# Weights behind the first preparation, its evictions on two engines, and a sort wait for every node-row DMA

## The chip, the cores and the metric

The kernel runs on one core of a Trainium2 chip. The metric is device time in microseconds, lower is better. The engines of the core are named PE (TensorE), DVE (VectorE), ACT (ScalarE), POOL (GpSimd) and SP (SyncE); each executes its own instructions in a fixed order, and waits for the others by semaphores.

## The reference

There are 16 graphs of 1024 nodes with 64 channels, and a dense 0/1 adjacency of each (about 16 neighbours a node). Two layers follow one another, both on normalized input. The first takes, for every node and channel, weighted quartiles over the node's remaining neighbours; the second is three graph convolutions.

```python
h = jnp.maximum(_layernorm(x, axis=-1), 0.0)
...
neigh = (adj_ > 0) & ~eye
...
skip = jnp.where(nb > T, (nb + K - 1) // K, 1)      # T, K = 10, 2
...
rem = neigh & (sk > 1) & (rank % sk == sk - 1) & mask[:, :, None]
rem = rem | jnp.swapaxes(rem, 1, 2)
adj_d = jnp.where(rem, 0.0, adj_)
nd = adj_d > 0
vals = jnp.where(nd[..., None], x[:, None, :, :], jnp.inf)
s = jnp.sort(vals, axis=2)
...
for tau, w in zip(TAUS, WTS):                       # quartiles 0.25, 0.5, 0.75
    ...
    agg = agg + jnp.asarray(w, x.dtype) * (v_lo + frac * (v_hi - v_lo))
...
h = jax.nn.relu(out @ W1 + b1)                      # out = x + agg
y = h @ W2 + b2
...
# second layer, adj undiminished
x1 = _bn(_gcn(x, adj, W1, b1), g1, be1, m1, v1)     # _gcn: relu(adj @ (x @ W) + b)
x2 = _bn(_gcn(x1, adj, W2, b2), g2, be2, m2, v2)
x3 = _bn(_gcn(x2, adj, W3, b3), g3, be3, m3, v3)
return jax.nn.relu(jnp.concatenate([x1, x2, x3], axis=-1) @ Wl + bl)
```

## The kernel before

The graphs are worked on in eight pairs. Three kinds of work follow one another for a pair.

*Preparation* (`prepare`, and `prepare_one` for each of its two graphs). The normalized rows are written to DRAM (h_d, and rows_d, which the node fetches read). Eight tiles of 128 rows of the adjacency are loaded by SyncE (L775, 512 KB each, two buffers), turned to fp8 by ScalarE with a count (edge, L782) and by VectorE (one, L786); PE transposes them (L789) and the result leaves PSUM as edgeT (L792, ScalarE). VectorE takes out the diagonal (L799), PE forms sums of every 128 columns (L757) and running counts (cs, L829 and L834), ScalarE and VectorE turn these into the removed edges (stays, L838 and L839), PE symmetrizes them (q, L849 to L860), and ScalarE evicts q as the remaining edges with the number of each node (L865). Nodes are then ordered by their number of neighbours: a key per node is spread over all partitions by PE (keys, L876), and eight comparisons with accumulation on ScalarE (L884) count how many keys lie above; `place` (L887) is the position. GpSimd scatters the edges' rows to their places in DRAM (live_d, L895) and reads them back (lp, L910), PE transposes them, ScalarE evicts (liveT, L933), and a list of source rows is drawn up: eight times row words on ScalarE (L988), a cast of every second pair (L993), and on VectorE the search for the largest numbers (L712, L714), which ends with rows_listed (L732). At the end the normalized rows are read again (h_again, L695) and split into three bf16 parts (hp, L697 to L700).

*Gathering and sorting.* The nodes in their new order are split into blocks. For most blocks PE gathers the neighbours' values by one-hot matrices that VectorE makes (s L1151 and L1216, pg L1176 and L1247), ScalarE evicts, and VectorE sorts them by a network of minima and maxima (L1092). For the three blocks of NODES, GpSimd fetches the neighbours' rows one slot at a time by indirect DMA (g_nodes, L1361, 744 in all); a DMA for a slot serves 128 nodes, and in one block there is one for each of `G` graphs or pairs, numbered by `a`.

*The layers* (`later`, `next_layer`). The sorted result goes through DRAM to its nodes' original order by indirect DMA of GpSimd (agg, L1554), VectorE adds it (L1451), and the two layers run on PE, ScalarE and VectorE (L1440 to L1532).

The order of the work is written by generators: `weave` interleaves the preparation of the next pair with the sorts of this one in shares (SHARES), and all layers with the sorts of the last pair (LATE_SHARES). The preparation of the first pair stands alone at the start: `ahead = Steps(prepare(0, early))`, `ahead.rest()`. From this program a list scheduler makes the fixed order of each engine; a dependency that carries no semaphore (NoSync) only constrains this order.

Ahead of the first preparation stand the constants. The weights are 48 DMAs, all issued by ScalarE (`weight`, `column`, `row`, `both`, L536 to L559), with three scale vectors made of them (bn_s, L571 to L577). GpSimd fills lines with values and sends them as a table of bounds (line L528, bounds L530, 32 DMAs). A tile `filler` with a zero row and a large row is set by VectorE (L623) in memory that the setup used before, and written by 16 ScalarE DMAs (L627) to the ends of rows_d.

A node-row DMA that is asked for during a sort gets a wait on the last instruction of that sort so far (`sorted_by`), but only for `a == 0`.

Of the kernel before, what the change touches and what calls it, by code (L numbers as in the profile page):

```python
# [10 lines left out]
F32 = mybir.dt.float32  # L11
# [397 lines left out]
def graph_layers_kernel(ctx: ExitStack, tc: tile.TileContext, ins, out: bass.AP):  # L409
# [126 lines left out]
    def weight(name, rows, cols, twice=False):  # L536
        t = const.tile([rows * (1 + twice), cols], F32, name=f"w_{name}")
        for k in range(1 + twice):
            nc.scalar.dma_start(out=t[k * rows : (k + 1) * rows, :], in_=ins[name])
        return t  # L540

    def column(name, rows, twice=False):
        t = const.tile([rows * (1 + twice), 1], F32, name=f"c_{name}")
        for k in range(1 + twice):
            nc.scalar.dma_start(out=t[k * rows : (k + 1) * rows, :], in_=ins[name].rearrange("(p o) -> p o", o=1))
        return t

    def row(name, cols):
        t = const.tile([P, cols], F32, name=f"r_{name}")
        nc.scalar.dma_start(out=t, in_=ins[name].partition_broadcast(P))  # L550
        return t

    def both(t, src):

        nc.vector.memset(t, 0.0)
        for k in range(2):
            half = slice(k * C, (k + 1) * C)
            nc.scalar.dma_start(out=t[half, half], in_=src)


    w1 = weight("L0_gnn_W1", C, HID, True)
    w2 = weight("L0_gnn_W2", HID, C)
    b1 = column("L0_gnn_b1", HID)
    b2 = row("L0_gnn_b2", C)
    layers = []
    for i in (1, 2, 3):
        wl = const.tile([P, P], F32, name=f"wl{i}")
        both(wl, ins[f"L1_gnn_W{i}"])
        bl, g, be, m, v = (column(f"L1_gnn_{k}{i}", C, True) for k in ("b", "g", "be", "m", "v"))
        s = const.tile([P, 1], F32, name=f"bn_s{i}")  # L570
        nc.vector.tensor_scalar(s, v, BN_EPS, None, ALU.add)  # L571
        nc.scalar.activation(s, s, AF.Sqrt)
        nc.vector.reciprocal(s, s)
        nc.vector.tensor_tensor(s, s, g, ALU.mult)

        nc.vector.tensor_tensor(m, m, s, ALU.mult)
        nc.vector.tensor_tensor(be, be, m, ALU.subtract)  # L577
        layers.append((wl, bl, s, be))
    wlast = const.tile([P, 3, P], F32, name="wlast")
    for i in range(3):  # L580
        both(wlast[:, i, :], ins["L1_gnn_Wl"][i * C : (i + 1) * C, :])
    blast = row("L1_gnn_bl", C)

# [37 lines left out]
    with tc.tile_pool(name="setup_fill", bufs=1) as setup:  # L621
        filler = setup.tile([2, C], F32, name="filler")
        nc.vector.memset(filler, BIG)  # L623
        nc.vector.memset(filler[:1, :], 0.0)
        for p in range(NP):
            for x in range(2):
                nc.scalar.dma_start(out=rows_d[p][x * ROWS + ZERO_ROW : x * ROWS + BIG_ROW + 1, :], in_=filler)  # L627

# [10 lines left out]
    def prepare(p, pools):  # L639
# [54 lines left out]
        for x in range(2):  # L694
            nc.sync.dma_start(out=h[:, x], in_=rows_of(h_d[2 * p + x][:, :]))  # L695
        st.hp = keep.tile([P, 3, 2, NT, C], BF16, tag="hp", name="hp")
# [68 lines left out]
    def prepare_one(st, x, pools, ahead=None):  # L765
        work, keep, ps = pools
        b = 2 * st.p + x
        mk = work.tile([P, NT], U8, tag="mk", name="mk")
        nc.sync.dma_start(out=mk, in_=mask_d[b])
# [10 lines left out]
        for t in range(NT):  # L780
            a, coming = coming, load(t + 1) if t + 1 < NT else None
            nc.scalar.activation(  # L782
                edge[:, t, :], a[:, :].bitcast(U32), AF.Sign, accum_out=found[:, 0, b, t : t + 1], saturate=False
            )
            one = work.tile([P, N], F8, tag="one", bufs=2, name="one")
            nc.vector.tensor_scalar(one, a, 1.0, None, ALU.is_equal, saturate=False)  # L786
            pt = ps.tile([P, NT, P], F32, tag="big", bufs=2, name="ptE")
            for u in range(NT):
                nc.tensor.matmul(  # L789
                    out=pt[:, u, :], lhsT=one[:, u * P : (u + 1) * P], rhs=ident_h, start=True, stop=True  # L790
                )
            nc.scalar.activation(  # L792
                edgeT[:, :, t * P : (t + 1) * P], pt, AF.Copy, accum_out=found[:, 1, b, t : t + 1], saturate=False
            )
            yield
# [48 lines left out]
        for t in range(NT):  # L844
            q = ps.tile([P, N], F32, tag="big", bufs=2, name="q")
            for hf in range(NH):
# [17 lines left out]

            nc.scalar.activation(  # L865
                edge[:, t, :], q, AF.Relu, bias=bias(-2.0), accum_out=nv[:, t : t + 1], saturate=False
            )
            yield
# [12 lines left out]

        junk = stays[:, 0, : N // 2].bitcast(F8)
        for t in range(NT):
            nc.scalar.activation(  # L884
                junk, keys, AF.Sign, bias=minus[:, t : t + 1], accum_out=above[:, t : t + 1], saturate=False
            )
        nc.vector.tensor_scalar(place[:, b, :], above, -0.5, 0.5 * (N - 1), ALU.mult, ALU.add)  # L887
# [34 lines left out]
        def find_live(lp_all, listed):  # L922
# [3 lines left out]
            for t in range(NT):  # L926
                lp = lp_all[:, t, :]
                pt = ps.tile([P, NT, P], F32, tag="big", bufs=2, name="pt")
                for u in range(NT):
                    nc.tensor.matmul(  # L930
                        out=pt[:, u, :], lhsT=lp[:, u * P : (u + 1) * P], rhs=ident_h, start=True, stop=True
                    )
                nc.scalar.activation(liveT[:, :, t * P : (t + 1) * P], pt, AF.Copy, saturate=False)  # L933
                yield
# [43 lines left out]
            for u in range(NT):  # L978
# [12 lines left out]
                if u % 2:  # L991
                    words = st.r[0][:, x, u - 1 : u + 1, :]
                    nc.scalar.copy(words, words.bitcast(BF16))  # L993
                    yield
# [353 lines left out]
    def fetch_nodes(pairs, i, pools, tag):  # L1348
# [7 lines left out]
        def ask():  # L1356
            for k in range(slots):
                for a in range(G):
# [7 lines left out]
                    )  # L1366
                    if a == 0 and sorted_by[0] is not None:
                        tc.add_manual_dep(
# [77 lines left out]
    def first_layer(pools, xt, h, agg, mask):  # L1446
# [7 lines left out]
        for x in range(X):  # L1454
            rows = slice(x * C, (x + 1) * C)
            hT = one.tile([HID, N], F32, tag="hT", name="hT")
            for hf in range(NH):
                sl = slice(hf * HALF, (hf + 1) * HALF)
                pm = ps.tile([HID, HALF], F32, tag="mm", name="pm1")
                nc.tensor.matmul(out=pm, lhsT=w1[rows, :], rhs=oT[rows, sl], start=True, stop=True)  # L1460
                nc.scalar.activation(hT[:, sl], pm, AF.Relu, bias=b1)
            py = ps.tile([P, NT, C], F32, tag="mm", name="py")
            for t in range(NT):
                nc.tensor.matmul(out=py[:, t, :], lhsT=hT[:, t * P : (t + 1) * P], rhs=w2, start=True, stop=True)  # L1464
            nc.vector.tensor_tensor(h[:, :, x, :], py, b2[:, None, :].to_broadcast([P, NT, C]), ALU.add)
            yield
# [7 lines left out]
    def next_layer(pools, graphs, adjT, x2, cur):  # L1474
# [6 lines left out]
        xs = []  # L1481
        for i, (wl, bl, s, be) in enumerate(layers):

# [35 lines left out]
        for hf in range(NH):  # L1519
            ts = slice(4 * hf, 4 * hf + 4)  # L1520
            pf = ps.tile([P, 4, X, C], F32, tag="mm", name="pf")
            for t in range(4):
                sl = slice((4 * hf + t) * P, (4 * hf + t + 1) * P)
                for i, xT in enumerate(xs):
                    nc.tensor.matmul(  # L1525
                        out=pf[:, t].rearrange("p x c -> p (x c)"), lhsT=xT[:, sl], rhs=wlast[:XC, i, :XC],
                        start=(i == 0), stop=(i == 2),
                    )
            nc.vector.tensor_tensor(
                res[:, ts], pf, blast[:, None, None, :].to_broadcast([P, 4, X, C]), ALU.add  # L1530
            )
# [212 lines left out]
    with ExitStack() as stack:  # L1744
# [6 lines left out]
        with ExitStack() as inner:  # L1751
# [4 lines left out]
            ahead = Steps(prepare(0, early))  # L1756
            ahead.rest()
            sts = [ahead.result]
            jobs = iter(NODE_ORDER)
# [132 lines left out]
```

## Time and profile before

| | |
|---|---|
| median of 3 runs | 2845.74 us (2841.83 to 2846.65) |
| the profiled execution, its own time | 2855.05 us |
| span of the profiled execution | 2853.2 us |
| mean granted TensorE clock | 0.869 |
| PE busy | 2127.4 us (75%), 21226 matmuls |
| DVE busy | 2259.9 us (79%), 5356 instructions |
| ACT busy | 1657.8 us (58%), 3324 |
| POOL busy | 1358.7 us (48%), 1155 |
| DMA traffic | 205.27 MB, mean 72 GB/s |

Times in the profile count from the start of the span. Busy time leaves out instructions that only issue a DMA on ACT and SP; these are shown on the engines' queues as ACTq and SPq. A row of a group gives its line, engine, operation, what it writes and reads, how many there are, busy time, the mean of one in ns, and the idle time of the engine just before them with what ended it. In the rows of slices a digit is a busy share in tenths.

### The profile page before, as it was taken

The numbers are of one execution on the slowest core, as the hardware profiler recorded it, in microseconds if no ns is written. First come the engines' busy times: TensorE is split into PE (matmuls) and PEld (weight loads), VectorE is DVE, ScalarE is ACT, GpSimd is POOL, SyncE is SP. The second block draws the span as 40 slices with busy tenths as digits, with TensorE's granted clock in tenths as the row PEclk, the third lists the DMA queues.
The fourth block names the chain that finished last, engine by engine and source line by source line (L and its number), as shares of the span: only waits on it lengthen the run. The fifth ranks groups of instructions, "written<-read, shape, count | busy, mean of one in ns | idle before, by whom it ended". The sixth has DMA issues, their size and how long they took to land. (4 is left out here: it accounts for less than half of the span.)

```text
span 2853.2 us, 54558 instructions
## 1 busy us (share of the span) xinstructions
PE 2127.4 (75%) x21226; PEld 1374.2 (48%) x21226; DVE 2259.9 (79%) x5356; ACT 1657.8 (58%) x3324; POOL 1358.7 (48%) x1155
## 2 busy tenths in 40 slices
PE   1567986897798699779855986997588496448768
PEld 0344563564455365545523553665355363234445
DVE  3117999889899989989999999989688486647843
ACT  2686788678677858867773777687423141122222
POOL 5115363475526416443734274175646748862220
PEclk9788997998899799789878997998798798778989
DMA  3303222322422323142431222322310351221221
GB/s 96 109 30 98 80 88 65 104 80 58 107 72 86 81 91 91 46 110 68 98 65 45 82 86 73 112 75 61 80 21 19 74 82 51 42 56 39 48 61 46
DMA packets 261035, 205.27 MB, mean 72 GB/s; under 512 B 217120, under 2 KB 217248, under 8 KB 256672
## 3 DMA queue, kind: packets, MB, share of 16 engines
q1 hardware_dynamic: 165120, 131.39, 15.5%
q0 software_dynamic: 39680, 62.23, 9.1%
q10 hardware_dynamic: 55968, 8.09, 2.1%
q8 instruction: 168, 2.75, 0.4%
q14 instruction: 99, 0.81, 0.1%
HBM read 148.82 MB, written 52.75 MB: 71 GB/s over the span
## 5 line engine op out<-in xcount | busy, mean ns | idle before, releaser
L1361 POOL DMA_INDIRECT g_nodes<-rows_d,rows_listed x744 | 979.2, 1316 | 952.5 <-DVE prod L1104 276.2
L1176 PE MATMUL pg<-s,hp 128*64 128x496 fp8e4 (+5 forms) x8064 | 747.0, 337 | 134.9 <-ACT hp L697 56.1
L1176 PEld LDWEIGHTS <-hp 128*64 128x64 bf16 x8064 | 450.2, 113 | 376.9 <-ACT hp L697 67.2
L1509 PE MATMUL pg<-adjT,xw 128*64 128x512 fp8e4 x2304 | 282.5, 394 | 24.6 <-ACT xw L1498 11.4
L895 POOL DMA_INDIRECT live_d<-edge,place x128 | 178.7, 1396 | 191.1 <-DVE place L887 154.9
L1151 DVE TENSOR_SCALAR s<-r 128x3200 uint16<-128x3200 uint16 (+2 forms) x192 | 199.6, 1049 | 56.9 <-PE pg L1176 56.8
L1554 POOL DMA_INDIRECT agg<-agg_d,place x128 | 134.8, 1053 | 196.4 <-DMA agg_d<-agg_nodes 118.0
L1509 PEld LDWEIGHTS <-xw 128*64 128x64 bf16 x2304 | 135.4, 113 | 154.1 <-issue 22.8
L782 ACT ACTIVATE edge<-a 128x1024 fp8e4<-128x1024 uint32 x128 | 135.8, 1062 | 105.1 <-DMA a<-in_adj 87.2
L1180 ACT ACTIVATE g<-pg 128x400 f32<-128x400 f32 (+3 forms) x168 | 84.3, 502 | 191.1 <-PE pg L1176 161.3
L1092 DVE TENSOR_TENSOR t<-g 128x800 f32<-128x800 f32 (+9 forms) x184 | 168.0, 926 | 5.4 <-ACT g L1180 3.4
L884 ACT ACTIVATE stays<-keys,minus 128x1024 fp8e4<-128x1024 f32 x128 | 143.6, 1122 | 41.7 <-PE keys L876 40.5
L865 ACT ACTIVATE edge<-q,bias 128x1024 fp8e4<-128x1024 f32 x128 | 142.2, 1112 | 41.6 <-PE q L860 41.6
L838 ACT ACTIVATE stays<-cs,back 128x1024 f16<-128x1024 f32 x128 | 139.1, 1114 | 41.5 <-DVE look L819 19.8
L789 PE MATMUL ptE<-ident_h,one 128*128 128x128 bf16 x1024 | 83.4, 232 | 106.1 <-DVE one L786 58.0
L1092 DVE TENSOR_TENSOR g<-t 128x992 f32<-128x992 f32 (+7 forms) x176 | 160.0, 934 | 2.4
L1451 DVE TENSOR_TENSOR agg<-agg,h_late 128x1024 f32<-128x1024 f32 x8 | 9.8, 1224 | 184.1 <-DMA agg<-agg_d,place 184.1
L930 PE MATMUL pt<-ident_h,lp 128*128 128x128 bf16 x1024 | 107.7, 276 | 60.7 <-ACT liveT L933 33.2
L1247 PE MATMUL pg<-s,hp 128*64 128x384 bf16 (+14 forms) x1872 | 149.1, 301 | 2.8 <-DVE s L1216 2.7
L792 ACT ACTIVATE edgeT<-ptE 128x1024 fp8e4<-128x1024 f32 x128 | 130.8, 1033 | 19.9 <-PE ptE L789 19.6
L1513 ACT ACTIVATE xT<-pg,c_L_gnn_b 128x512 f32<-128x512 f32 x48 | 32.9, 686 | 183.9 <-PE pg L1509 175.3
L786 DVE TENSOR_SCALAR one<-a 128x1024 fp8e4<-128x1024 f32 x128 | 88.5, 696 | 55.6 <-DMA a<-in_adj 45.3
(253 smaller groups left out, 5043.3 us busy)
## 6 DMA issues: line engine op xcount, KB each, us to landing
a<-in_adj SPq DMA_DIRECT2D x128, 512.0 KB
adjT_d<-edgeT SPq DMA_DIRECT2D x16, 1024.0 KB
lp<-live_d POOLq DMA_DIRECT2D x32, 512.0 KB
adjT<-adjT_d SPq DMA_DIRECT2D x16, 1024.0 KB
g_nodes<-rows_d,rows_listed POOLq DMA_INDIRECT x744
room<-in_x SPq DMA_DIRECT2D x16, 256.0 KB
h_d<-room SPq DMA_DIRECT2D x16, 256.0 KB
rows_d<-room SPq DMA_DIRECT2D x64, 64.0 KB
```

The lines of the kernel that those rows point to most:

```text
L782: nc.scalar.activation(edge[:, t, :], a[:, :].bitcast(U32), AF.Sign, accum_out=found[:, 0, b, t : t + 1], saturate=False)
L838: nc.scalar.activation(stays[:, t, :], cs, AF.Abs, bias=back[:, t : t + 1], scale=2.0)
L865: nc.scalar.activation(edge[:, t, :], q, AF.Relu, bias=bias(-2.0), accum_out=nv[:, t : t + 1], saturate=False)
L884: nc.scalar.activation(junk, keys, AF.Sign, bias=minus[:, t : t + 1], accum_out=above[:, t : t + 1], saturate=False)
L895: sent = nc.gpsimd.indirect_dma_start(out=live_d[b][:, :], out_offset=bass.IndirectOffsetOnAxis(ap=place[:, b, t : t + 1], axis=0), in_=ed ...
L1092: sorted_by[0] = nc.vector.tensor_tensor(view(bufs, o, n1, n2), view(bufs, a, n1, n2), view(bufs, b, n1, n2), ALU.max if op else ALU.min)
L1151: nc.vector.tensor_scalar(s[:, j, :, us, :], st.r[0][:, :, us, j0:j1], abs(k - 3), 0x0808, ALU.logical_shift_right if k > 3 else ALU.logic ...
L1176: summed = nc.tensor.matmul(out=pg[x * C : (x + 1) * C, those, :], lhsT=st.hp[:, part, x, u, :], rhs=picked, start=(i == 0 and part == 0), ...
L1247: summed = nc.tensor.matmul(out=pg[x * C : (x + 1) * C, ks, w0:], lhsT=st.hp[:, part, x, u, :], rhs=s[:, ks, x, u, w0:], start=(whole and ...
L1361: asked = nc.gpsimd.indirect_dma_start(out=g[:, k, a * C : (a + 1) * C], out_offset=None, in_=rows_d[st.p][:, :], in_offset=bass.IndirectO ...
L1509: nc.tensor.matmul(out=pg[cs, :], lhsT=part[:, u, cs], rhs=adjT[x][:, u, sl], start=(u == 0 and k == 0), stop=(u == NT - 1 and k == len(xw ...
L1554: nc.gpsimd.indirect_dma_start(out=agg[:, t, x, :], out_offset=None, in_=agg_d[b][:, :], in_offset=bass.IndirectOffsetOnAxis(ap=place[:, b ...
```

## The change

The weights are loaded by SyncE and no longer at the start: `load_weights` is called behind the preparation of the first pair, and each of its DMAs has a dependency without semaphore on the last read of h_again, so the scheduler places it behind that one. The three scale vectors move with them. The DMAs of the filler rows go from ScalarE to GpSimd. In the preparation of the first pair alone (`shared`), edgeT is evicted by VectorE, every second tile of q, every second comparison of keys and every second tile of liveT go to VectorE (with a second scratch half, junk_2), and so do the casts of the row words. The comparisons on VectorE count by `is_gt` and not by a sign, and one more small instruction brings their result to the same scale. Last, every node-row DMA, not only that of `a == 0`, waits for the sort's instruction. The diff, cut to its core:

```diff
@@ the weights
     def weight(name, rows, cols, twice=False):
...
-            nc.scalar.dma_start(out=t[k * rows : (k + 1) * rows, :], in_=ins[name])
+            load_one(t[k * rows : (k + 1) * rows, :], ins[name])
...
+    read_last = [None]
+
+    def load_one(to, source):
+
+        load = nc.sync.dma_start(out=to, in_=source)
+        tc.add_manual_dep(
+            load.ins, read_last[0].ins.name,
+            mybir.DependencyInfo(mybir.DependencyClass.NoSync, mybir.DependencyReason.SCHED_ONLY),
+            reason="weights are wanted late",
+        )
...
+    def load_weights():
...
+        for i in (1, 2, 3):
...
+            nc.vector.tensor_scalar(s, v, BN_EPS, None, ALU.add)
+            nc.scalar.activation(s, s, AF.Sqrt)
+            nc.vector.reciprocal(s, s)
+            nc.vector.tensor_tensor(s, s, g, ALU.mult)
...
@@ the filler rows
-                nc.scalar.dma_start(out=rows_d[p][x * ROWS + ZERO_ROW : x * ROWS + BIG_ROW + 1, :], in_=filler)
+                nc.gpsimd.dma_start(out=rows_d[p][x * ROWS + ZERO_ROW : x * ROWS + BIG_ROW + 1, :], in_=filler)
@@ prepare
         for x in range(2):
-            nc.sync.dma_start(out=h[:, x], in_=rows_of(h_d[2 * p + x][:, :]))
+            read_last[0] = nc.sync.dma_start(out=h[:, x], in_=rows_of(h_d[2 * p + x][:, :]))
@@ prepare_one
+        shared = st.p == 0
...
-            nc.scalar.activation(
-                edgeT[:, :, t * P : (t + 1) * P], pt, AF.Copy, accum_out=found[:, 1, b, t : t + 1], saturate=False
-            )
+            if shared:
+                nc.vector.tensor_scalar(
+                    edgeT[:, :, t * P : (t + 1) * P], pt, 1.0, 0.0, ALU.mult, ALU.add,
+                    accum_out=found[:, 1, b, t : t + 1], saturate=False,
+                )
+            else:
...
+            if shared and t % 2:
+                nc.vector.tensor_scalar(
+                    edge[:, t, :], q, 2.5, 0.0, ALU.is_ge, ALU.add, accum_out=nv[:, t : t + 1], saturate=False
+                )
+            else:
...
+            if shared and t % 2:
+                nc.vector.tensor_scalar(
+                    junk_2, keys, key[:, t : t + 1], 0.0, ALU.is_gt, ALU.add, accum_out=above[:, t : t + 1],
+                    saturate=False,
+                )
+            else:
...
+                if shared and t % 2:
+                    nc.vector.tensor_copy(liveT[:, :, t * P : (t + 1) * P], pt, saturate=False)
+                else:
...
+                    if shared:
+                        nc.vector.tensor_copy(words, words.bitcast(BF16))
+                    else:
+                        nc.scalar.copy(words, words.bitcast(BF16))
@@ fetch_nodes
-                    if a == 0 and sorted_by[0] is not None:
+                    if sorted_by[0] is not None:
@@ the main sequence
             ahead = Steps(prepare(0, early))
             ahead.rest()
+            load_weights()
```

## The prediction

> **What bounds the kernel now.** I read the page's 40 slices first (71.3 us each), then a stretch table of the first 250 us, then the timeline and the waits around the start, the groups, and last the waits of VectorE and the POOL rows of the end.
>
> ```profile
> PE   1567986897798699779855986997588496448768
> DVE  3117999889899989989999999989688486647843
> ACT  2686788678677858867773777687423141122222
> POOL 5115363475526416443734274175646748862220
> PEclk9788997998899799789878997998798798778989
> ```
>
> Three regimes. From slice 4 to about slice 28 (285 to 2000 us) DVE is at 8 to 9 tenths: it is the bound, about 248 us a pair. In the last 850 us DVE and PE alternate, with waits between. In slices 2 and 3, the first pair's preparation, DVE is at 1, and PE at 5 and 6: nothing overlaps with it, so what ends it late starts everything late. The stretch table (columns: PE, PEld, DVE, ACT, POOL busy with counts, clock, DMA share, GB/s) shows who sets it:
>
> ```profile
> 60.00:77.00 17.00, 2.07 (x16) 1.64 (x17) 2.77 (x4) 10.79 (x20) 0.00 (x0) 1.00 0.63 211
> ...
> 163.00:173.00 10.00, 0.49 (x8) 0.37 (x6) 0.17 (x1) 9.77 (x17) 0.00 (x0) 0.65 0.00 0
> ...
> 197.00:207.00 10.00, 7.41 (x72) 5.89 (x72) 0.00 (x0) 8.91 (x10) 0.00 (x0) 0.67 0.00 0
> 207.00:227.00 20.00, 11.79 (x96) 5.92 (x95) 14.93 (x66) 18.22 (x40) 0.00 (x0) 0.76 0.13 28
> ```
>
> ScalarE is the bound from 163 to 207; from 207 on VectorE (list of rows, L712/L714) is nearly as full. Before 60 us it is neither, but one chain; timeline rows (start, length, engine, line, operation, in brackets the idle before):
>
> ```profile
> 31.66 0.59 ACTq L550 DMA_DIRECT2D r_L_gnn_bl<-in_L_gnn_bl  x1
> 32.30 1.06 ACT L603 ACTIVATE room<-room 128x1024 f32<-128x1024 f32 x1 [1.73 <-DMA wlast<-in_L_gnn_Wl]
> ...
> 55.66 0.11 DVE L623 MEMSET filler<- 2x64 f32 x1 [13.86 <-DMA bounds<-line]
> ...
> 56.03 5.05 ACTq L627 DMA_DIRECT2D rows_d<-filler  x16
> 61.13 1.06 ACT L782 ACTIVATE edge<-a 128x1024 fp8e4<-128x1024 uint32 x1 [17.08 <-DMA rows_d<-filler]
> ```
>
> ScalarE first issues 48 weight DMAs (0.77 to 32.25 us, 0.62 us each) and only then does its first work. Then VectorE stands 13.86 us at the filler's memset, whose memory is free only when POOL's table of bounds has been sent (its last issue is at 54.05); ScalarE stands behind the filler's DMAs. The first graph's diagonal step (L799) runs at 77.02, and all of its sums follow.
>
> **The change, part by part.** After the first pair's preparation the order of instructions on PE, VectorE, ScalarE and SyncE is that of before; only POOL's is changed throughout. So there are four terms.
>
> *A. The start.* The 48 issues leave ScalarE; edgeT of this pair (L792) goes to VectorE; the filler's DMAs go to POOL. The adjacency loads, 512 KB at the 211 GB/s of the row above, come about every 2.5 us, so sixteen are there by about 45 us. VectorE's memset still waits for the bounds, but now lies just ahead of the diagonal step, behind the tiles of graph 0 and two of graph 1: it hides them. POOL's chain begins some 2 us later in the new order, so the bounds end near 57.5, the diagonal step comes near 58.5 in place of 77.02: -18.5 us. If the chain slips 4 us further, -14; if it does not slip, -21. Here a rule speaks against the change: the Trainium skill, "DMA: Bandwidth & Descriptors", section "Issuing engines are not separate DMA queues", says that all issuers share 16 DMA engines and another issuer saves only sequencer time, usually small beside the transfer. By it the move is worth nothing. The row says that the sequencer's time is what counts: 48 issues fill ScalarE to 32.25, while the inputs' rows wait. But of those 32 us only the part not covered by the bounds' chain is gained, so neither 32 nor 0 stands in the sum.
>
> *B. Evictions shared.* ScalarE's prices: 1.11 plus 0.19 for the read of the accumulator (L865, L884), 1.03 (L933), 1.27 (L993, 128x1280).
> - keys of graph 1: eight at 1.24 us pitch, 162.86 to 172.6, with PE and DVE empty. Halved: -4.7.
> - liveT, twice eight at about 1.04. Halved, PE at 0.6 to 0.95 a tile becomes the bound: -2 each, -4.
> - the four casts L993 of graph 0's row words: ScalarE alternates 2 x 0.8 and 1.27; without casts 8 x 0.8, PE's pace some 1.0: -3.5.
> - q, both graphs: PE feeds a tile in 1.3 to 1.4 us, so -1.2 each, -2.4; sums and the overlap of graph 0's keys with graph 1's edgeT: -1.5.
> Together -16. VectorE is then busier where it was nearly full (14.93 of 20 us): four casts of graph 1 there, nearest row L839, 128x1024 f16 at 0.49, so 0.6 each for 1280: +2.5. B is -13.5, between -18 (all halves overlap) and -7 (VectorE's share exposed).
>
> VectorE's f32 reads out of PSUM with 1024 elements are not in the trace. The nearest form, L786 from SBUF, takes 0.69; the nearest source, L1529 with 512 elements out of PSUM, takes 0.68, so 1.2 for 1024, as L602's 1024 f32 from SBUF do (1.21). The Trainium skill ("VectorE: DVE Perf Modes", "Why PSUM operands drop a tier") says that such a source loses the doubled rate, which speaks for 1.2. By 0.69 or by 1.2 the sum is the same where four go to each engine, since ScalarE's four take 5 us; only above 1.3 does VectorE set the pace. What the accumulation adds is unknown, 0 to 0.2 us an instruction: at 0.2, 2 us.
>
> *C. The weights behind.* 48 DMAs, at 0.62 us about 29.7 us of SyncE, now after the two h_again issues (227.46). Behind them on SyncE stand the room's h_d and rows_d of pair 1 (5.4 us of issues) and its adjacency loads:
>
> ```profile
> 227.46 0.99 SPq L695 DMA_DIRECT2D h_again<-h_d  x2
> ...
> 242.17 47.96 SPq L775 DMA_DIRECT2D a<-in_adj  x9
> ```
>
> Before, these nine went out over 48 us, held by buffers. Afterwards the first comes near 267, bunched at 2.5 us; VectorE meets its first one near 273, so the cover is thin: 2 to 8 us, I take 5. In VectorE's order the three bn constants wait for the 17th, 29th and 41st DMA (+14, +21, +29 us after the list) between the first gather's L1216 steps: the first two hidden, the third 3 us late. C is +8, from +2 to +14.
>
> *D. POOL.* The group of the 744 node-row DMAs (busy, mean ns, then POOL's idle time before them), and VectorE's waits from 2000 us on (total, times, longest):
>
> ```profile
> L1361 POOL DMA_INDIRECT g_nodes<-rows_d,rows_listed x744 | 979.2, 1316 | 952.5 <-DVE prod L1104 276.2
> ```
>
> ```profile
> DVE agg L1451 <- DMA agg<-agg_d,place: 184.1, 8, 61.5
> ```
>
> Only the first half of each pair of node blocks waited for its sort; the second ran ahead in bursts. Now both stand in line at the sort, with live_d (L895), lp and agg (L1554) queued behind them, and the sort of the next node block waits for the rows. I laid the new order on the old times of what each waits for, 1.62 us a node DMA (1.32 and the usual 0.3 of gap), 1.35 an agg (1.05 and 0.3), 2 us to land. In the middle, rows come after VectorE wants them in pairs 0/1 (sort at 786, +10.5), near 1410 (+4.5) and at 2087 (+16, counted in the end); the first two mostly stand, with small ones elsewhere: +11, from 0 to +25. At the end VectorE's 184.1 us of waits for agg change by where agg stands in POOL's line: the first is 7.5 sooner, the second 9.3 later net of the late sort, then 2.5, 20.3, 20.1 and 9.9 sooner, but once POOL has node DMAs left it is POOL itself that gives the pace, and only the last difference remains: -10, from -18 to -4. D is +1.
>
> **Sum:** -18.5 - 13.5 + 8 + 1 = -23 us. The profiled execution took 2855.05 (span 2853.2), 0.3% over the median of 2845.74; the difference is taken as it is: 2845.74 - 23 = 2823.
>
> **Rivals.**
> - *Late node rows (slower).* The place: the node sorts of the eight pairs (L1092, t_nodes from g_nodes). The waits are now between an engine that is full (VectorE at 9) and a queue that must start after it. Four more sorts have under 5 us of margin in my layout. A to C and the end give -34; it decides against the change from a mean of 4.3 us a pair. At 6 a pair, 8 x 6 - 34 = +14: 2860. For: DVE is the bound and has no slack. Against: POOL is 48% busy and three places only are late by the layout. 0.17.
> - *The weights stand in pair 1's way.* VectorE waits for the third constant in full and then for every load: C is +25, so 2840. For: VectorE's queue is in order. Against: the DMA engines' share is 0.3 there. 0.12.
> - *The end keeps 20 us* (the fourth and fifth agg's gains stay): -43, 2803. For: 184.1 us of waits. Against: POOL full from 2354 to 2530. 0.15.
> - *The change does not do what it says at the start*: the bounds set it alone, A at -14 and B at -7: -12, 2834. 0.10.
>
> **How the numbers follow.** The likeliest, 2823, has 0.46. About 0.2% (5.7 us) is what a measurement of this kernel can tell from no change. The first rival is the slower side (0.17, with 0.02 from the second); the second lies about the bound (0.05 same); the others are faster, less 0.02 same: faster 0.74, same 0.07, slower 0.19. The range takes the end's gain (2803) as its low side, and +2 us on the median as its high side, 2848, leaving out about 0.05 below and 0.15 above.
>
> **What would show it.** A: the diagonal step of graph 0 near 58.5, the first node-row DMA (227.71 before) near 196. B: under 6 us for graph 1's keys; VectorE's PSUM evictions of 1024 near 1.2. C: SyncE with 48 issues from about 196; VectorE waiting on adjacency loads and c_L_gnn_v for some 8 us in the next 60. D: new VectorE waits on g_nodes of 5 to 16 us near 790 and 2090 in old times; the agg waits down from 184 by 10 to 40. I am wrong if the diagonal step is over 65, if SyncE's weights delay pair 1 by more than 15, or if the waits for g_nodes total over 35 us.

## The result, and the profile after

The changed kernel takes 2864.65 us (median of 5 runs, 2857.09 to 2867.01), the kernel before 2845.74 us: a ratio of 1.0063, interval 1.0042 to 1.0084. It is slower by 19 us. The forecast was 2823 us. The profiled execution took 2864.35 us, span 2862.6. Line numbers are now those of the changed kernel: L1361 became L1407, L1092 became L1138, L1451 became L1497, L799 became L825.

The busy slices of the page after (71.6 us each):

```profile
PE   2658986996788699779745895997577696456868
DVE  4557998999799889989899899899677688556843
ACT  3455778578567858867683588587523132121222
POOL 6115454373627336453805383455555748872220
```

VectorE is at 5 and 5 in slices 2 and 3, where it was at 1 and 1: it has the shared work. From slice 29 on its row looks like the one before, a little later. The start, from the timeline of VectorE:

```profile
60.35 0.11 DVE L642 MEMSET filler<- 2x64 f32 x1 [16.97 <-DMA bounds<-line]
60.53 0.11 DVE L643 MEMSET filler<- 1x64 f32 x1
60.57 0.35 DVE L825 TENSOR_TENSOR edgeT<-edgeT,off_diag 128x256 int32<-128x256 int32 x1
```

The diagonal step of graph 0 runs at 60.57 in place of 77.02, straight behind the wait for the bounds. That part came as forecast. The weights on SyncE, behind the list of rows:

```profile
212.99 0.99 SPq L714 DMA_DIRECT2D h_again<-h_d  x2
214.03 1.85 SPq L565 DMA_DIRECT2D w_L_gnn_W<-in_L_gnn_W  x3
...
245.21 0.59 SPq L565 DMA_DIRECT2D r_L_gnn_bl<-in_L_gnn_bl  x1
...
252.48 27.11 SPq L795 DMA_DIRECT2D a<-in_adj  x10
```

The loads of pair 1 go out in 27 us where they had 48. The longest waits of VectorE over the whole span (total, times, longest):

```profile
DVE agg L1497 <- DMA agg<-agg_d,place: 163.6, 8, 65.3
...
DVE t_nodes L1138 <- DMA g_nodes<-rows_d,rows_listed: 34.8, 4, 14.7
DVE top L731 <- ACT listed L1015: 27.4, 11, 6.9
DVE one L806 <- DMA a<-in_adj: 22.6, 23, 4.0
...
DVE bn_s L590 <- DMA c_L_gnn_v<-in_L_gnn_v: 9.2, 3, 5.1
```

The second row is new: before, VectorE never waited for a node row. Where it does, in VectorE's timeline:

```profile
786.35 1.49 DVE L1138 TENSOR_TENSOR t_nodes<-g_nodes 128x1280 f32<-128x1280 f32 x1 [10.01 <-DMA g_nodes<-rows_d,rows_listed]
...
1422.16 1.49 DVE L1138 TENSOR_TENSOR t_nodes<-g_nodes 128x1280 f32<-128x1280 f32 x1 [10.71 <-DMA live_d<-edge,place]
...
1607.99 1.23 DVE L1138 TENSOR_TENSOR t_nodes<-g_nodes 128x1024 f32<-128x1024 f32 x1 [8.19 <-DMA g_nodes<-rows_d,rows_listed]
...
2111.76 1.49 DVE L1138 TENSOR_TENSOR t_nodes<-g_nodes 128x1280 f32<-128x1280 f32 x1 [14.66 <-DMA g_nodes<-rows_d,rows_listed]
```

(The second is named by a scatter that ended last; the tile waited for is the same, so the waits for node rows are 45.5 us and not 34.8.) What GpSimd does ahead of the first of these sorts, before (L1361) and after (L1407):

```profile
759.53 1.41 POOL L1361 DMA_INDIRECT g_nodes<-rows_d,rows_listed  x1 [16.68 <-DVE g L1092]
...
776.30 1.19 POOL L1361 DMA_INDIRECT g_nodes<-rows_d,rows_listed  x1 [0.30 <-issue]
```

```profile
749.91 1.41 POOL L1407 DMA_INDIRECT g_nodes<-rows_d,rows_listed  x1 [11.92 <-DVE g L1138]
...
782.72 0.94 POOL L1407 DMA_INDIRECT g_nodes<-rows_d,rows_listed  x1 [0.30 <-issue]
```

Before, 11 DMAs were left when the wait for the sort ended, and the last was sent at 777.5; after, 22 were left, and the last was sent at 783.7, too late for VectorE, which was free at 776.3. From about 375 us on VectorE's instructions stand in the same order in both kernels (ahead of that some neighbours of pair 1's preparation change places), so the difference in start time of one and the same instruction shows where the lead went:

| instruction on VectorE | before, us | after, us | after - before |
|---|---|---|---|
| diagonal step, graph 0 | 77.0 | 60.6 | -16.5 |
| rows_listed, graph 1 | 227.2 | 212.7 | -14.5 |
| agg of pair 0's first block | 293.4 | 281.9 | -11.5 |
| list of rows, pair 2 (L712) | 708.5 | 700.2 | -8.4 |
| node sort after the first late rows | 786.4 | 786.3 | 0.0 |
| after the second | 1410.7 | 1422.2 | +11.5 |
| after the third | 1589.4 | 1608.0 | +18.6 |
| first agg of the end | 2052.8 | 2063.8 | +11.0 |
| node sort at the fourth | 2086.7 | 2111.8 | +25.1 |
| fourth agg | 2375.4 | 2375.5 | +0.2 |
| sixth agg | 2593.3 | 2605.3 | +12.0 |
| last rows compared | 2734.5 | 2743.8 | +9.3 |

A lead of 11.5 us at 282 turns into a lag of 18.6 us at 1608: 30 us lost, most of it in three steps of 8 to 11 us, each at a node sort. These are two single executions, and that of the kernel before lies 9.3 us above its own median; by the medians the lag at the end is 19 us and not 9.

### The profile page after: what moved, and what is told of

It is laid out like the page before. It is cut to its first block, busy times and chain, and to the rows that moved or that the text cites. A ratio compares the mean times of both kernels' runs of the same rounds, so it can differ in the third digit from the quotient of the medians.

```text
span 2862.6 us, 54538 instructions
## 1 busy us (share of the span) xinstructions
PE 2134.3 (75%) x21226; PEld 1372.9 (48%) x21226; DVE 2313.3 (81%) x5438; ACT 1609.3 (56%) x3245; POOL 1380.8 (48%) x1171
## 5 line engine op out<-in xcount | busy, mean ns | idle before, releaser
L1407 POOL DMA_INDIRECT g_nodes<-rows_d,rows_listed x744 | 1018.4, 1369 | 984.4 <-DVE g L1138 303.6
L1222 PE MATMUL pg<-s,hp 128*64 128x496 fp8e4 (+5 forms) x8064 | 756.0, 339 | 160.6 <-DVE s L1197 65.9
L1555 PE MATMUL pg<-adjT,xw 128*64 128x512 fp8e4 x2304 | 279.5, 392 | 23.5 <-ACT xw L1544 11.5
L1197 DVE TENSOR_SCALAR s<-r 128x3200 uint16<-128x3200 uint16 (+2 forms) x192 | 199.4, 1048 | 45.3 <-PE pg L1222 42.0
L935 POOL DMA_INDIRECT live_d<-edge,place x128 | 153.5, 1199 | 134.6 <-issue 64.1
L1138 DVE TENSOR_TENSOR t<-g 128x800 f32<-128x800 f32 (+9 forms) x184 | 167.9, 926 | 5.4 <-ACT g L1226 3.4
L1138 DVE TENSOR_TENSOR t_nodes<-g_nodes 128x256 f32<-128x256 f32 (+6 forms) x192 | 124.7, 659 | 48.6 <-DMA g_nodes<-rows_d,rows_listed 34.8
L922 ACT ACTIVATE stays<-keys,minus 128x1024 fp8e4<-128x1024 f32 x120 | 134.5, 1121 | 49.0 <-PE keys L907 37.5
L1138 DVE TENSOR_TENSOR g<-t 128x992 f32<-128x992 f32 (+7 forms) x176 | 160.0, 934 | 2.4
L896 ACT ACTIVATE edge<-q,bias 128x1024 fp8e4<-128x1024 f32 x120 | 133.2, 1111 | 48.9 <-PE q L886 48.9
L970 PE MATMUL pt<-ident_h,lp 128*128 128x128 bf16 x1024 | 104.3, 270 | 60.4 <-ACT liveT L976 29.7
L1497 DVE TENSOR_TENSOR agg<-agg,h_late 128x1024 f32<-128x1024 f32 x8 | 9.9, 1231 | 163.6 <-DMA agg<-agg_d,place 163.6
L976 ACT ACTIVATE liveT<-pt 128x1024 fp8e4<-128x1024 f32 x120 | 117.1, 1033 | 25.2 <-PE pt L970 19.1
```

The lines of the kernel that those rows point to most:

```text
L896: nc.scalar.activation(edge[:, t, :], q, AF.Relu, bias=bias(-2.0), accum_out=nv[:, t : t + 1], saturate=False)
L922: nc.scalar.activation(junk, keys, AF.Sign, bias=minus[:, t : t + 1], accum_out=above[:, t : t + 1], saturate=False)
L935: sent = nc.gpsimd.indirect_dma_start(out=live_d[b][:, :], out_offset=bass.IndirectOffsetOnAxis(ap=place[:, b, t : t + 1], axis=0), in_=ed ...
L1138: sorted_by[0] = nc.vector.tensor_tensor(view(bufs, o, n1, n2), view(bufs, a, n1, n2), view(bufs, b, n1, n2), ALU.max if op else ALU.min)
L1197: nc.vector.tensor_scalar(s[:, j, :, us, :], st.r[0][:, :, us, j0:j1], abs(k - 3), 0x0808, ALU.logical_shift_right if k > 3 else ALU.logic ...
L1222: summed = nc.tensor.matmul(out=pg[x * C : (x + 1) * C, those, :], lhsT=st.hp[:, part, x, u, :], rhs=picked, start=(i == 0 and part == 0), ...
```

## The experiments

Two theories. Theory 1: the added waits on the a == 1 half make node rows late. Theory 2: the earlier start and the weights shift GpSimd's order, and the waits are harmless.

The experiments fell on five chips. On two of them the kernel before takes 3210 us, not 2845. What is different there is told first, since it turns a verdict round. Some of the expectations call such a chip "starved". No chip was used twice, so whether it is the chip itself or its state at that time stays open.

**The first four kernels, where before takes 3212.43 us.**

The half waits undo the third part of the change, the waits alone are the third part:

```diff
 # e1_half_waits: the changed kernel
-                    if sorted_by[0] is not None:
+                    if a == 0 and sorted_by[0] is not None:
 # e2_waits_only: the kernel before
-                    if a == 0 and sorted_by[0] is not None:
+                    if sorted_by[0] is not None:
```

> The changed kernel, with the wait on the sort back on the a == 0 half of the node-row DMAs alone. Theory 1 (the waits put node rows late at the sorts near 786, 1411 and 1589 of the time before, about 27 us, and the end gives back a few): the lead of 11 us that VectorE has at 293 us stays to the end, 2832 to 2837. Theory 2 (the order of POOL is shifted by the weights and the earlier start, not by the waits): the late rows stay, 2855 to 2865.

> The kernel before, with the wait on every node-row DMA and nothing else changed. Theory 1: VectorE waits for node rows at the same three sorts and the end takes some of it back, so 15 to 25 us slower, 2861 to 2871. Theory 2: 2843 to 2849.

No sharing is the half-waits kernel with one line changed; sharing alone is the kernel before with the hunks of `prepare_one`:

```diff
 # e3_weights_only: e1, and
-        shared = st.p == 0
+        shared = False
 # e4_sharing_only: the kernel before, and
+        shared = st.p == 0
 ...
```

> Weights on SyncE behind the first preparation and the filler's DMAs on GpSimd, alone: evictions all on ScalarE, waits on the a == 0 half. If sharing the evictions is worth next to nothing, as the stage times of the changed kernel say (keys in turns, q and liveT at PE's pace), the same as the run with the half waits within 4 us, 2832 to 2839. If sharing is worth the 13.5 us of the prediction, 2845 to 2850.

> The kernel before with the first pair's evictions shared, alone: weights first on ScalarE, filler rows on ScalarE, waits on the a == 0 half. If the sharing gives next to nothing: 2840 to 2848. If it gives the prediction's 13.5: 2830 to 2834.

| kernel | median, us | ratio to before | interval |
|---|---|---|---|
| e1 half waits | 3207.83 | 0.9977 | 0.9959 to 0.9995 |
| e2 waits only | 3111.29 | 0.9698 | 0.9647 to 0.9749 |
| e3 no sharing | 3205.63 | 0.9982 | 0.9959 to 1.0006 |
| e4 sharing only | 3214.14 | 1.0006 | 0.9988 to 1.0023 |

None of the expectations had this. The waits alone make the kernel 3% faster here. The stretch table of e4, from the first node-row DMAs on (PE, PEld, DVE, ACT, POOL busy with counts, clock, DMA share, GB/s), shows what differs:

```profile
245.00:265.00 20.00, 8.33 (x47) 2.99 (x43) 0.00 (x0) 0.19 (x2) 15.10 (x17) 0.65 0.25 73
```

and about the same work in a half-waits kernel on a chip of the other kind (h1, below):

```profile
226.00:246.00 20.00, 18.48 (x248) 12.75 (x244) 9.39 (x23) 4.91 (x13) 15.73 (x15) 1.00 0.19 33
```

The half-waits kernel itself was run on a chip of the first kind too (f1, below); these are the 20 us that lie about as far behind its first node-row DMA as those of h1:

```profile
228.70:248.70 20.00, 5.18 (x31) 2.28 (x28) 0.48 (x3) 0.12 (x1) 15.12 (x17) 0.67 0.20 30
```

While GpSimd issues node-row DMAs back to back, PE gets through 31 matmuls in 20 us and not 248, and VectorE through 3 instructions and not 23. Over the whole of f1 VectorE is busy for 58% of the time in which GpSimd sends eight or more indirect DMAs with pauses under 0.4 us, and for 81% of the rest (counted from the trace); in h1 it is 81% and 82%. VectorE's instructions themselves are no slower: its busy time is 2313.9 us in f1 and 2312.8 in h1. PE's rows in e4 name no engine as the cause:

```profile
249.01 0.54 PE L1203 MATMUL pg<-s,hp 128*64 128x400 fp8e4 x4 [0.94 <-issue]
...
251.15 1.22 PE L1203 MATMUL pg<-s,hp 128*64 128x400 fp8e4 x4 [1.59 <-issue]
...
253.28 0.82 PE L1203 MATMUL pg<-s,hp 128*64 128x400 fp8e4 x3 [0.92 <-issue]
```

A few matmuls at a time, then a pause in which nothing that the trace shows is waited for. The DMA share is 0.20 in f1 and 0.19 in h1, so full transfer engines are not the reason. It looks as if the engines were short of instructions while GpSimd runs its indirect DMAs, but that is not shown. The profile's queue of instruction loads (packets, MB, share of the engines' span) does not tell the two kinds apart; it reads the same in e4 and in the kernel before:

```profile
q8 instruction: 168, 2.75, 0.4%
```

The cause stays open. Waiting for the sort at both halves breaks GpSimd's runs apart, and that is worth 3% there: the waits are all that e2 changes, and with them (f0, below) VectorE is busy for 72% of GpSimd's runs and not 58%.

**Once more, with the changed kernel beside them.** This again fell on a chip of that kind (before 3209.93 us).

> The changed kernel once more, beside the three below, because the four runs before it were on a chip where the kernel before took 3212 us and all engines stood still[...] while GpSimd sent its DMAs back to back. Theory 1, with that effect told apart: where the kernel before takes about 2845 us, the changed one takes 1.004 to 1.008 of it; where it takes about 3200 us, the waits break up GpSimd's bursts and the changed kernel takes about 0.965 of it (the waits alone 0.970, the rest 0.998).

> The changed kernel with the wait on the a == 0 half alone. Where before takes about 2845: theory 1, 2832 to 2837 (the lead of 11 us at 293 us stays); theory 2 (POOL's order is spoilt by the earlier start and the weights, not by the waits), 2855 to 2865. Where before takes about 3200: 0.996 to 1.000 of it, as the time before.

> The kernel before with the wait on every node-row DMA, nothing else. Where before takes about 2845: theory 1, 2861 to 2871, with VectorE's waits on node rows at three sorts; theory 2, 2843 to 2849. Where before takes about 3200: 0.965 to 0.975 of it.

The fourth takes away what the filler waits for, by giving it memory of its own:

```diff
 # f3_filler_apart: f1, and
-    with tc.tile_pool(name="setup_fill", bufs=1) as setup:
-        filler = setup.tile([2, C], F32, name="filler")
+    if True:
+        filler = const.tile([2, C], F32, name="filler")
```

> The run with the half waits, and the filler tile in memory of its own, so that its memset doesn't wait for the bounds. The diagonal step of graph 0 comes after the eighth adjacency tile, near 40 us in place of 60.6: if the start is what sets everything after it, 15 to 20 us less than the run with the half waits, 2814 to 2821 where before takes 2845. If pair 1's weights and loads take the lead back, within 5 us of it.

| kernel | median, us | ratio to before | interval |
|---|---|---|---|
| f0 changed | 3105.59 | 0.9652 | 0.9596 to 0.9707 |
| f1 half waits | 3201.73 | 0.9969 | 0.9951 to 0.9988 |
| f2 waits only | 3107.68 | 0.9687 | 0.9651 to 0.9722 |
| f3 filler apart | 3191.00 | 0.9949 | 0.9931 to 0.9967 |

The changed kernel is 3.5% faster on this chip, and 0.6% slower on that of the recorded result. Even here one count does not depend on the chip: VectorE's waits on g_nodes are 26 to 28 us in each of e2, f0 and f2, which have all the waits, and none in e1, e3, e4, f1 and f3. In f2:

```profile
DVE t_nodes L1092 <- DMA g_nodes<-rows_d,rows_listed: 27.5, 4, 14.7
```

So theory 1's mechanism is there, hidden under a larger effect of the opposite sign. The diagonal step comes at 45.3 in f3 and at 60.7 in f1, and the time falls by 10.7 us.

**Where before takes 2854.08 us.** If late rows are the cost, asking sooner must take it away with the waits left in. The main sequence gives the part of a node block's slots that is asked for in the sort ahead:

```diff
 # g1_asks_sooner: the changed kernel
-                weave(sort_block(st, 1, pools), asking(nodes, 0.1, 1.0, 0.4), steps(2))
+                weave(sort_block(st, 1, pools), asking(nodes, 0.1, 1.0, 0.8), steps(2))
 ...
-                    asking(nodes, 0.0, 1.0, 0.4),
+                    asking(nodes, 0.0, 1.0, 0.8),
 # g2_and_filler: g1, and the filler as in f3
 # g3_and_two_keys: g2, and
+        keys_2 = keys
+        if shared:
+            keys_2 = ps.tile([P, N], F32, tag="big", bufs=2, name="keys_2")
 ...
-                    junk_2, keys, key[:, t : t + 1], 0.0, ALU.is_gt, ALU.add, accum_out=above[:, t : t + 1],
+                    junk_2, keys_2, key[:, t : t + 1], 0.0, ALU.is_gt, ALU.add, accum_out=above[:, t : t + 1],
```

> The changed kernel, as the point of reference for the three below on the same chip: about 0.965 of the time before where before takes about 3210 us, 1.004 to 1.008 where it takes about 2845. VectorE's waits for node rows 25 to 36 us in total.

> The changed kernel with its waits, but 0.8 in place of 0.4 of the slots of a node block asked for during the sort ahead (pairs' middle blocks, and block 1), so that GpSimd's last row is asked for earlier. Theory 1 (the last rows are late because the waits hold back all 34 DMAs of a block until the sort before it has begun, and GpSimd then needs 1.5 to 2.1 us for each): VectorE's waits for node rows fall from about 27 to under 8 us, and the time by 15 to 25 us against the changed kernel. Rival (the rows are late because GpSimd or the transfers are too slow in all): they stay over 20 us and the time within 6 us. What speaks against a gain: more DMAs in a row[...], up to +30 us.

> The run with sooner asks, and the filler tile in memory of its own: the diagonal step near 45 us in place of 60.6, so 10 to 16 us less than the run with sooner asks. If the starved engines hide it, within 4 us of it.

> The run before this one, and the keys written twice by PE, into two PSUM tiles, one for ScalarE's comparisons and one for VectorE's. If two engines that read one PSUM tile are made to take turns (in the changed kernel 1.28 us on VectorE, then 1.3 on ScalarE, 10.3 us for eight), the eight comparisons of graph 1 take 5 to 6 us and PE's second writing 2: 2 to 4 us less in all. If the turns come from elsewhere, the comparisons stay at 10 us and the time rises by about 2.

| kernel | median, us | ratio to before | interval | VectorE on g_nodes, us |
|---|---|---|---|---|
| g0 changed | 2871.49 | 1.0052 | 1.0032 to 1.0072 | 34.5 |
| g1 asks sooner | 2846.38 | 0.9974 | 0.9959 to 0.9989 | 11.6 |
| g2 and filler | 2832.72 | 0.9920 | 0.9890 to 0.9949 | 10.5 |
| g3 and two keys | 2831.65 | 0.9921 | 0.9903 to 0.9939 | 12.5 |

The recorded result comes again in g0; with the sort that is named by a scatter its waits for node rows are 45.2 us. Asking sooner takes 25.1 us off and leaves 11.6 us of the waits, at the same pace of GpSimd (1.38 us a node-row DMA in g0, 1.35 in g1): it is the late start that makes the rows late. Asking sooner was not tried without the added waits; but g1 does not get below the half-waits kernel (h1 below, 0.9953), so nothing shows a gain beyond theirs. The filler's own memory gives another 13.7 us.

g3 settles why the keys gained nothing. In the changed kernel the two engines take turns, by its timeline:

```profile
147.19 1.28 DVE L917 TENSOR_SCALAR_CACHE_REDUCE stays<-keys,key 128x1024 fp8e4<-128x1024 f32 x1 [3.17 <-ACT stays L922]
...
148.52 1.11 ACT L922 ACTIVATE stays<-keys,minus 128x1024 fp8e4<-128x1024 f32 x1 [1.36 <-DVE stays L917]
...
149.75 1.28 DVE L917 TENSOR_SCALAR_CACHE_REDUCE stays<-keys,key 128x1024 fp8e4<-128x1024 f32 x1 [1.27 <-ACT stays L922]
```

With a PSUM tile for each they run side by side, in g3:

```profile
141.23 1.28 DVE L925 TENSOR_SCALAR_CACHE_REDUCE stays<-keys,key 128x1024 fp8e4<-128x1024 f32 x1 [3.73 <-PE keys L915]
...
142.56 1.28 DVE L925 TENSOR_SCALAR_CACHE_REDUCE stays<-keys,key 128x1024 fp8e4<-128x1024 f32 x1
```

The eight comparisons of graph 1 last 7.1 us (139.44 to 146.5) in g3 and 10.2 (132.36 to 142.6) in g2. Each engine's turn begins when the other's read ends, and with a tile for each this wait is gone, while an instruction takes as long as before (1.28 and 1.11 us): the turns are a wait of the program for the tile that both read. The time isn't less, though. The diff shows that the second tile takes the other of the two buffers of its tag (`bufs=2`), and graph 1's transposes need one too. They begin at 77.00 in g2 and at 81.54 in g3:

```profile
81.54 0.61 PE L809 MATMUL ptE<-ident_h,one 128*128 128x128 bf16 x8 [3.22 <-ACT stays L930]
```

Graph 1's diagonal step is at 110.2 in place of 102.7.

**The parts apart, where before takes 2848.11 us.**

> The changed kernel with the wait on the a == 0 half alone, for a chip on which the engines aren't starved (before about 2850). Theory 1 (the added waits cost 25 to 30 us in the middle and give back some at the end): 11 us under the kernel before, 0.995 to 0.998. Theory 2 (the earlier start and the weights spoil GpSimd's order): 1.003 to 1.007, as the whole change. On a starved chip again 0.996 to 0.999.

> The kernel before with all the waits, nothing else. Not starved: theory 1, 1.005 to 1.010, with 25 to 36 us of VectorE waits for node rows; theory 2, within 0.999 to 1.001. Starved: 0.965 to 0.975.

> The weights and the filler's DMAs moved, nothing shared, waits on the a == 0 half. If sharing the evictions gives nothing, within 3 us of the run with the half waits; if it gives the 13.5 us of the prediction, 10 to 16 us more than that run.

> The run with the half waits, and the filler in memory of its own. If the bounds' chain still holds the start, and nothing behind it takes the lead back: 10 to 16 us less than the run with the half waits, 0.991 to 0.994 of the time before. If the weights and pair 1's loads take it back: the same as that run within 4 us.

The edits are those of e1, e2, e3 and f3.

| kernel | median, us | ratio to before | interval |
|---|---|---|---|
| h1 half waits | 2833.26 | 0.9953 | 0.9931 to 0.9974 |
| h2 waits only | 2869.98 | 1.0074 | 1.0047 to 1.0101 |
| h3 no sharing | 2819.97 | 0.9920 | 0.9896 to 0.9945 |
| h4 filler apart | 2820.52 | 0.9913 | 0.9886 to 0.9941 |

Theory 1 is right, theory 2 falls: the waits alone cost 22 us, and without them the rest of the change is 15 us faster than before. In h2, VectorE's waits are

```profile
DVE t_nodes L1092 <- DMA g_nodes<-rows_d,rows_listed: 38.1, 5, 14.7
```

and the lag against the trace of before is 14.7 us at the sort at 786, 29.3 at 1411, 35.6 at 1589, and 23.1 at the end. What I had not expected is h3: without the sharing the kernel is 13.3 us faster than with it. The intervals of h1 and h3 overlap a little (0.9931 to 0.9974, 0.9896 to 0.9945), so the size is uncertain. Two more pairs of runs differ in the sharing alone: h4 and k1, and g2 and k2 (k1 and k2 below). By the ratios they give 16 and 15 us in the same direction, and their intervals do not overlap. The stage times, as starts of the instruction named, show the direction too:

| us | before | changed | h1 half waits | h3 no sharing | h4 filler apart | k1 |
|---|---|---|---|---|---|---|
| diagonal step, graph 0 | 77.0 | 60.6 | 60.7 | 46.2 | 45.5 | 42.6 |
| place, graph 0 | 123.3 | 104.3 | 103.8 | 101.3 | 90.2 | 89.5 |
| diagonal step, graph 1 | 132.9 | 116.2 | 115.5 | 110.9 | 102.2 | 99.1 |
| place, graph 1 | 172.8 | 156.4 | 155.4 | 150.2 | 142.4 | 138.4 |
| last liveT | 204.9 | 185.5 | 186.2 | 182.8 | 171.5 | 171.1 |
| rows_listed | 227.2 | 212.7 | 211.8 | 204.8 | 198.6 | 193.2 |

Without edgeT on VectorE the scheduler puts the diagonal step ahead of the filler's memset (46.2), and the next VectorE work behind it (60.26). Set h4 beside k1 (the same but for the sharing): sharing costs 4 us up to graph 1's place (2.9 of them are there at graph 0's diagonal step, with edgeT on VectorE), wins 3.6 over the liveT stage, and loses 5.1 from there to rows_listed, where VectorE makes the list of rows and now the casts too. That is 5.4 us of the 9 to 16; the rest was not located, and some us of it can be noise. For in the kernels with half waits the lead over before at rows_listed (15.3 us in h1, 22.3 in h3, 28.5 in h4, 34.0 in k1) is about what is left of it at the end, by the medians (14.9, 28.1, 27.6 and 37.7).

**The start without sharing, with both kinds of waits, where before takes 2849.41 us.**

```diff
 # k1_best: f3, and
-        shared = st.p == 0
+        shared = False
 # k2_all_waits_sooner: g2, and the same line
```

> Nothing shared, waits on the a == 0 half, weights moved, filler in memory of its own: the no-sharing run (0.992 of before) and the filler's 12.7 us (0.0045) together, if the two gains add: 0.986 to 0.989 where before takes 2850. If the no-sharing run's start already hides the filler's wait, 0.991 to 0.993. On a starved chip, 0.992 to 0.997.

> The same start, but with all the waits and the sooner asks: by the runs before (sooner asks and filler with sharing 0.992, half waits and filler with sharing 0.9913) about equal to the first, 0.986 to 0.991 where before takes 2850; on a starved chip 0.955 to 0.965, since it still breaks up GpSimd's bursts.

k1 takes 2811.68 us, ratio 0.9857 (0.9833 to 0.9881); k2 2811.25 us, ratio 0.9866 (0.9843 to 0.9889). Both beat the kernel before by 1.3 to 1.4%, and so, by the ratios to before, the changed one by about 2%. The gains of the filler and of dropping the sharing add. k2 keeps the waits that break up GpSimd's runs, which is what the chips of the first eight runs reward; k2 was not run on one of them.

## Why the prediction was wrong

A to C were to give -24 us together and gave -14.9 (h1). D was to cost 1 us and cost 22 (the waits alone, h2) to 31 (the changed kernel against h1, by the ratios): this turned the sign.

- **A, the start: -18.5.** Right in mechanism and nearly in size: -16.5 at the diagonal step. ScalarE's first tile is at 7.15 us now, where its first work was at 32.30, so it was the time of ScalarE's queue that the weights had cost, as the sum had it. The chain of bounds ends 4.7 us later (55.66 to 60.35), where 2 was put into the sum and 6 was the worst case named. That this chain was the limit was right (f3, g2, h4: 10.7 to 13.7 us more when it is taken out of the way).
- **B, evictions: -13.5. The step that failed first, with the wrong sign.** The three pairs of runs that differ in the sharing alone give +9, +15 and +16 us by the ratios. By the stages (h4 against k1), the terms up to graph 1's place were to give -8.6 and cost 4.0, liveT and the row words were to give -7.5 and gave -3.6, and the end was to cost 2.5 and cost 5.1. The keys (-4.7) assumed that two engines read one PSUM tile at once: eight took 10.2 us, against 9.8 on ScalarE alone. q (-2.4) stood at PE's pace already: eight tiles take 11.1 us before and 11.2 after. And edgeT on VectorE, for which B had no price, puts graph 0's diagonal step 2.9 us later. VectorE's durations themselves were right: 1.22 us for a 1024 eviction out of PSUM, where 1.2 was written, and 0.49 for a cast, where 0.6 was.
- **C, the weights behind: +8.** Too dear. In h1 the lead falls from 15.3 us at rows_listed to 12.0 at 281 us and is 14.7 at 443: 3 us, then regained. The constants' waits of 9 to 11 us are there, but other waits shrink. A and C without B (h3) were put at -10.5 and gave -28 by the medians, -23 by the ratios.
- **D, the added waits: +1. The step that decided the sign.** The late places were found: 10.01 us where 10.5 was written, 14.66 where it was 16. One was missed altogether (8.19 at 1608), one was 10.7 and not 4.5. The layout gave every node DMA the mean of 1.62 us, and 2 us to land. Ahead of 786 and 2087, where the forecast held, 22 DMAs go out at 1.56 and 1.55 us, and VectorE starts 2.7 and 2.6 us behind the last. Ahead of 1608 one DMA alone takes 9.52 us and 34 take 71 us, not the 55 of the mean, and VectorE starts 7.4 us behind the last:

```profile
1529.67 3.84 POOL L1407 DMA_INDIRECT g_nodes<-rows_d,rows_listed  x1 [97.43 <-DVE g_pairs L1138]
...
1548.05 9.52 POOL L1407 DMA_INDIRECT g_nodes<-rows_d,rows_listed  x1 [0.30 <-issue]
...
1599.51 1.11 POOL L1407 DMA_INDIRECT g_nodes<-rows_d,rows_listed  x1 [0.30 <-issue]
```

In the stretch between the last DMA and VectorE's start, the share of the transfer engines (the column before the last) is 0.63 there and 0.23 at 786:

```profile
1600.60:1607.90 7.30, 4.14 (x43) 2.25 (x40) 0.00 (x0) 2.75 (x6) 0.02 (x1) 1.00 0.63 222
...
783.70:786.30 2.60, 0.00 (x0) 0.00 (x0) 0.00 (x0) 0.00 (x0) 0.00 (x0) 1.00 0.23 40
```

These are 21 us that the layout did not have, for a wait of 8.2. At 1422 it is the same in small: 28 DMAs at 1.81 us (two other loads lie between them), and 6.1 us behind the last. The trace of before has a DMA of 8.39 us near the same place, at 1539.24; why single ones are that long was not looked into.

The middle costs 30 us in the changed kernel, 35.6 in h2, not 11; in h2 9 us of that are small drifts between the waits. At the end the changed kernel wins 9.3 us from its lag at 1608, and h2 12.5; the forecast was 10. But h1, without the added waits, also gains 13 us over the same end, so this gain can't be put down to them. All three are set against the one traced execution of before, which is 9.3 us slower than its median, and that may be most of the gain; it was not settled.

- The first rival had the mechanism and the price: late node rows at VectorE's sorts, decisive from a mean of 4.3 us a pair, 2860 us. The measured 30 us are 3.8 a pair over eight; with B's failure that is enough. It was given 0.17. My argument against it, GpSimd's 48%, is an average: what counts is the time between the end of the wait and the sort that wants the rows. Ahead of 786 it was 26.4 us (749.9 to 776.3), and the 22 DMAs still open took 33.8; ahead of 1608 it was 70 us, and the 34 DMAs took 71 us and their rows 7.4 more.
- Of the signs named, three came against the forecast: graph 1's keys took 10.2 us and not under 6, the first node-row DMA went out at 213.2 and not near 196, and the waits for node rows were 45.5 us, over the 35 that was to mean that the forecast is wrong.

## What to carry to other kernels

A wait that holds back requests takes away their head start even where the engine that sends them is half idle: count the requests still open when the wait ends, times their pace at that place and not its mean, and the time to land, against the time to their use, and do it for every place where it occurs, not for the worst two. Sharing an eviction between two engines gives nothing where both read one tile, or where the engine that feeds them sets the pace, and its price is paid where the second engine is full later on. Before moving work off a chain, look for a false dependency on it: a 512-byte tile in reused memory was worth nearly as much (12.7 us, h4 against h1) as the whole rearrangement of the start (14.9, h1 against before).

## What the runs showed of the hardware

The same kernel takes 2845 to 2854 us on some chips and 3210 on others. On the latter PE, ScalarE and VectorE stand nearly still while GpSimd issues indirect DMAs in a row (31 matmuls in 20 us and not 248, f1 against h1), and there GpSimd itself is no slower: its node-row DMAs take 1.27 us in the mean in f1 and 1.32 in h1. On such a chip the changed kernel is 3.5% faster than the kernel before, on the others 0.5 to 0.6% slower. A comparison that is to hold has to say on which kind it was made.
